# One exponential for three late score tiles of a pair, and the first heads' loads spread over the projections, in a four-layer graph network

## The chip, the cores and the metric

The kernel runs on one core of a Trainium2 chip. The metric is the device time of one execution in microseconds; the time before is 11191.26 us, the median of three runs (11190.45 to 11191.84).

## The reference

`x` is [3327, 128] and `adj` a 0/1 matrix [3327, 3327]. Four layers follow each other, each as `x = x + layer(relu(layernorm(x)), adj)`. Layer 1, a graph attention with 128 heads of 8 features, takes most of the time:

```python
q = (x @ Wq.T).reshape(d, n, h)      # d = 128 heads, n = 3327, h = 8
k = (x @ Wk.T).reshape(d, n, h)
v = (x @ Wv.T).reshape(d, n, h)
a = jnp.einsum('dnh,dmh->dnm', q, k) * scale
a = a + spatial_encoding + edge_encoding      # both are adj
a = jax.nn.softmax(a, axis=2)
out = jnp.einsum('dnm,dmh->dnh', a, v)
out = out.reshape(n, h * d)
return out @ Wo.T
```

So each head has a 3327 x 3327 matrix of scores, to which twice `adj` is added before the exponential. The other layers are products with `adj`, a GRU cell and a nearest-neighbour step.

## The kernel before, in words

**Projections (lines 421 to 510).** For each of 26 row blocks of 128 nodes TensorE multiplies by Wq, Wk and Wv (L464, L471), ScalarE copies each result into a staging tile (`qk_st` L466, `v_st` L474), and SP's queue stores it to memory (`store`, L440). The heads are taken in 32 groups of four. For the first groups `Parting` (L359 on) reads q and k back, splits each value into a rounded high part and a rest on GpSimd, and stores both parts (`kt`, `qt`), so that a score can be a product of 32 contraction rows: high and low parts of eight features. A list `early` holds such steps; after each row block from the third on one step is taken from it. Among them stand, as one step each, the loads of the first group (`load_heads(0, 0)`: eight times `k_in` and `q4`, then four times `v4`), and all 13 exponentials of `adj` (`exp_of`, L347), and then the steps that rearrange keys (`key_pair`, L419). Each `v_st` gets its column of ones by a GpSimd memset (L473). In this part a scheduler places the instructions; the program's order is not kept.

**Attention (lines 519 to 631).** The query nodes are cut in 7 chunks of 476 (the last 471). For each chunk and each group of four heads, 26 row tiles t of 128 keys are gone through; a `step` is one (chunk, group, t). The order here is written by hand (`manual_schedule`) and kept by every engine.

In `scores` each step makes four tiles [128 keys, up to 476 queries], one for each head, by matmuls on the four row groups of 32 rows of the array (L547). Twice `adj` comes in by one of three ways, a letter for each head:

```python
WAYS = ("DDDI", "DDIG")            # for even and odd t
PLACES = ((0, 1, 2, 5), (3, 4, 6, 7))
```

D: VectorE adds `a2` (twice adj) to the scores and writes to `p8` (L552); these scores are in tiles `early`, one PSUM bank each, four buffers. I: TensorE adds it in PSUM by a matmul with twice the identity (L550). G: GpSimd multiplies the exponential by the exponential of twice adj, `e_a` (L555). I and G scores are in a tile `late`, read by ScalarE's exponential (L553). An even step has one late score (tile `late1`, one bank), an odd step two (`late2`, two banks). After an odd step one wide exponential goes over the five D places of the pair (L557), in place. `p8` has eight places of 476 for a pair of steps and three buffers.

`weigh` (L564) multiplies each tile of `p8` by the values, on the four column groups, and adds up in one PSUM bank `acc` over t; each fp32 product is two matmul instructions, so a step has eight. It runs four steps behind the scores (`ahead = 4`). After the last t VectorE copies `acc` out (L573). PSUM is full: `acc` 1 bank, `late1` 1, `late2` 2, `early` 4.

On TensorE a step stands as: late scores, early scores, identity, the weighing of four steps ago. Beside it, in t 4 to 25, run the loads of the next group on SP's queue and its key rearrangement on GpSimd.

Of the kernel before, what the change touches and what calls it, by code (L numbers as in the profile page):

```python
# [8 lines left out]
F32 = mybir.dt.float32  # L9
# [18 lines left out]
E = 8  # L28
# [26 lines left out]
def kernel(  # L55
# [285 lines left out]
    def even(c):  # L341
        w = q_chunks[c][1]
        return w + w % 2

    def exp_of(a2, c):
        e = e_pool.tile([P, QW], F32, name="e")
        nc.scalar.activation(e[:, : even(c)], a2[:, : even(c)], AF.Exp)  # L347
        return e
# [40 lines left out]
                if t == 11:  # L389
                    self.store(side)  # L390

    def load_heads(c, g):
        q0, w = q_chunks[c]
        k_in = kq.tile([P, NP], F32, name="k_in", bufs=1)
        q4 = kq.tile([P, QW], F32R, name="q4")
        v4 = kq.tile([P, 4, T, EA], F32, name="v4")
        nc.gpsimd.memset(k_in[:, N:], 0.0)
        if w % 2:
            nc.gpsimd.memset(q4[:, w : w + 1].bitcast(F32), 0.0)
        for i in range(4):  # L400
# [5 lines left out]
        for i in range(4):  # L406
            n0 = (4 * g + i) * N
            nc.sync.dma_start(
                v4[:, i].rearrange("p t e -> p (t e)"),
                vd[n0 : n0 + NP, :].rearrange("(p t) e -> p (t e)", t=T),  # L410
            )
        return k_in, q4, v4, []

    def key_pair(heads):
# [7 lines left out]
    with tc.tile_pool(name="l1", bufs=1) as pool, tc.tile_pool(name="l1_ps", bufs=3, space=PSUM) as ps:  # L422
        w_st = pool.tile([D, 3, NH * E], F32, name="w_st")
        for i, w in enumerate((wq, wk, wv)):
            nc.gpsimd.dma_start(w_st[:, i, :], w)
        zero = pool.tile([HL, NH], F32, name="zero")
        nc.vector.memset(zero, 0.0)
        nc.gpsimd.dma_start(vd[N * NH : N * NH + 1, :], zero[:1, :EA])
        for end in (qf, kf):
            nc.gpsimd.dma_start(end[:E, N * NH :], zero[:E])  # L430

        with tc.tile_pool(name="l1_ln", bufs=1) as ln, tc.tile_pool(name="l1_tp", bufs=2, space=PSUM) as tps:
            h, done = layernorm_relu(ln)
            done(T)
            hT = transposed(pool, tps, h, "hT")
        st = ctx_st.enter_context(tc.tile_pool(name="l1_st", bufs=4))

        def store(dst, src, r, kp):
            for p0, p1 in ((0, kp),) if kp == P else ((0, 112), (112, kp)):
                nc.sync.dma_start(dst[r * P + p0 : r * P + p1], src[p0:p1])  # L440


        assert 7 * N + NP <= 2 * P * NH
        early = []
        for g in range(2):
            part = Parting(g)
            for side in range(2):
                early.append(lambda part=part: (part.load(0), part.load(1)) if part.lo[0] is None else None)
                early.append(lambda part=part, side=side: [part.part(side, i) for i in range(4)] and part.store(side))
        first, e_first = [], []  # L450
        early.append(lambda: first.extend(load_heads(0, 0)))
        ahead_part = Parting(2)
        early.append(lambda: (ahead_part.load(0), ahead_part.load(1)))
        early.append(lambda: e_first.extend(exp_of(a, 0) for a in a_first[1::2]))
        early += [lambda: (key_pair(first), key_pair(first))] * (T // 4)
        if T // 2 % 2:
            early.append(lambda: key_pair(first))
        for r in range(T):
            kp = rows_of(r)
            lhs = hT[:, r * P : r * P + kp]  # L460
            for i, (dst, mx) in enumerate(((qf, q_max), (kf, k_max))):
                pp = ps.tile([P, 2, 512], F32, name="pp", bufs=2)
                for c in range(2):
                    nc.tensor.matmul(pp[:kp, c, :], lhs, w_st[:, i, c * 512 : c * 512 + 512], start=True, stop=True)  # L464
                s = st.tile([P, E * NH], F32, name="qk_st")
                nc.scalar.activation(s[:kp], pp[:kp].rearrange("p a b -> p (a b)"), AF.Copy, scale=D**-0.5 if i == 0 else 1.0)  # L466
                nc.vector.tensor_reduce(mx[:kp, r : r + 1], s[:kp], AX.X, ALU.max, apply_absolute_value=True)
                store(dst[:E].rearrange("e (r c) -> r e c", c=NH), s.rearrange("p (e c) -> p e c", c=NH), r, kp)
            pp = ps.tile([P, 2, 512], F32, name="pp", bufs=2)
            for c in range(2):  # L470
                nc.tensor.matmul(pp[:kp, c, :], lhs, w_st[:, 2, c * 512 : c * 512 + 512], start=True, stop=True)  # L471
            s = st.tile([P, NH, EA], F32, name="v_st")
            nc.gpsimd.memset(s[:, :, E : E + 1], 1.0)  # L473
            nc.scalar.copy(s[:kp, :, :E], pp[:kp].rearrange("p a (c e) -> p (a c) e", e=E))  # L474
# [44 lines left out]
    with tc.tile_pool(name="at_in", bufs=1) as a_pool, tc.tile_pool(name="at_p", bufs=3) as p_pool, tc.tile_pool(  # L519
# [13 lines left out]
            q0, w = q_chunks[c]  # L533
            nc.sync.dma_start(adj16[t][:, q0 : q0 + w], a2[:, :w])

        def scores(step, heads, a2, e_a, p8):
            c, _, t = step
            we = even(c)
            _, q4, _, pairs = heads
            ways, places = WAYS[t % 2], PLACES[t % 2]  # L540
            n_d = ways.count("D")
            late = ps.tile([P, 4 - n_d, 512], F32, name=f"late{4 - n_d}")
            early = [ps.tile([P, 512], F32, name="early", bufs=4) for _ in range(n_d)]
            for i in (*range(n_d, 4), *range(n_d)):
                r = slice(32 * i, 32 * i + 32)
                sp = early[i] if i < n_d else late[:, i - n_d]
                nc.tensor.matmul(sp[:, :we], pairs[t // 2][r, t % 2, :], q4[r, :we], start=True, stop=ways[i] != "I")  # L547
            for i in range(4):
                if ways[i] == "I":
                    nc.tensor.matmul(late[:, i - n_d, :we], two_i, a2[:, :we], start=False, stop=True)  # L550
            for i in range(n_d):
                nc.vector.tensor_tensor(p8[:, places[i], :we], early[i][:, :we], a2[:, :we], op=ALU.add)  # L552
            nc.scalar.activation(p8[:, places[n_d] : places[3] + 1, :we], late[:, :, :we], AF.Exp)  # L553
            if ways[3] == "G":
                nc.gpsimd.tensor_tensor(p8[:, places[3], :we], p8[:, places[3], :we], e_a[:, :we], op=ALU.mult)  # L555
            if t % 2:
                nc.scalar.activation(p8[:, :5, :we], p8[:, :5, :we], AF.Exp)  # L557

        def weigh(step, v4, p8):
            c, g, t = step  # L560
# [17 lines left out]
        with tc.manual_schedule(engines=engines):  # L578
# [7 lines left out]
            for j, step in enumerate(steps):  # L586
# [6 lines left out]
                        a_t, a_next = a_next, []  # L593
                        e_t, e_next = e_next, []
                if t % 2 == 0:
                    p8 = p_pool.tile([P, 8, QW], F32, name="p8")
                scores(step, heads, a_t[t], e_t[t // 2], p8)
                begun[j] = (step, heads[2], p8)
                if j >= ahead:
                    weigh(*begun.pop(j - ahead))  # L600
                if t == min(4, T // 2) and more:
                    coming = load_heads(*groups[n])
                if c == 0 and g + 2 < n_groups:
# [506 lines left out]
```

## Time and profile before

| | |
|---|---|
| median of the runs | 11191.26 us |
| the profiled execution | 11195.14 us |
| its span, first to last instruction | 11193.4 us |
| granted TensorE clock, mean | 0.989 |
| busy: TensorE / ScalarE / VectorE / GpSimd | 97% / 91% / 83% / 54% |
| VectorE's adds (L552) | 14560, 646 ns each |
| ScalarE's wide exponentials (L557) | 2912, 2599 ns each |
| ScalarE's late exponentials (L553) | 5824, 1378 ns of 952 elements, 971 ns of 476 |
| TensorE's weighing (L564) | 46592 instructions, 564 ns each |

Times come from one profiled execution. PE is TensorE, PEld its weight loads, DVE VectorE, ACT ScalarE, POOL GpSimd and SP the queue that issues transfers. A line gives the source line, the engine, the operation, output<-input with partitions x elements, how often it ran, and then the busy time in us and the mean of one in ns, and the idle time before it with what ended that. In the timeline the first column is the start, the second how long the merged instructions took. Instructions of one engine overlap in these records: the next starts before the last has ended, so the pace of an engine is read from start to start.

### The profile page before, as it was taken

The page shows a single profiled execution, that of the slowest core. Times are in us where ns is not written, and L with a number is a line of the kernel's source. Part 1 is how long each engine was busy: PE and PEld are TensorE (multiplying, and loading weights), DVE is VectorE, ACT ScalarE, POOL GpSimd, SP SyncE. Part 2 cuts the span into 40 slices and gives each one's busy share as a digit, 9 for nine tenths or more (in the row PEclk, how much of TensorE's full clock was granted, in tenths as well). Part 3 has the DMA queues.
Part 4 walks back from the last instruction along what each step waited for, and adds up shares of the span by engine and source line. Part 5 has one row for each costly group of instructions (what it writes and reads, how often), then busy time and mean ns, then how long its engine had stood idle before and what let it go on. Part 6 is the DMA issues. An engine that isn't in the chain of part 4 may idle for free. (4 is left out here: it accounts for less than half of the span.)

```text
span 11193.4 us, 209350 instructions
## 1 busy us (share of the span) xinstructions
PE 10850.5 (97%) x79530; PEld 3005.9 (27%) x79530; DVE 9343.1 (83%) x15429; ACT 10199.3 (91%) x9152; POOL 6016.3 (54%) x6964
## 2 busy tenths in 40 slices
PE   9899999999999999999999999999999999999996
PEld 4322222222222222222222222222222222222453
DVE  8588888888888888888888888888888888888656
ACT  0399999999999999999999999999999999999522
POOL 0277777555555555555555555555555555555203
PEclk9899999999999999999999999999999999999998
DMA  7755554333333333333333333333333332333432
GB/s 264 238 129 120 123 127 109 65 64 64 68 64 62 67 66 63 68 65 61 68 66 63 66 66 61 67 66 61 66 66 61 66 63 55 61 58 58 135 113 97
DMA packets 417541, 942.25 MB, mean 84 GB/s; under 512 B 67936, under 2 KB 345937, under 8 KB 380940
## 3 DMA queue, kind: packets, MB, share of 16 engines
q1 hardware_dynamic: 412762, 918.98, 37.4%
q8 instruction: 627, 10.27, 0.4%
q0 software_dynamic: 3760, 9.78, 0.3%
q14 instruction: 392, 3.21, 0.1%
HBM read 788.78 MB, written 139.71 MB: 83 GB/s over the span
## 5 line engine op out<-in xcount | busy, mean ns | idle before, releaser
L552 DVE TENSOR_TENSOR p<-early,a 128x476 f32<-128x476 f32 (+1 forms) x14560 | 8426.4, 646 | 1369.4 <-PE early L547 1297.5
L557 ACT ACTIVATE p<-p 128x2380 f32<-128x2380 f32 (+1 forms) x2912 | 7568.4, 2599 | 0.4
L564 PE MATMUL acc<-p,v 128*9 128x476 f32 (+1 forms) x46592 | 5748.5, 564 | 15.3 <-ACT p L557 1.4
L553 ACT ACTIVATE p<-late 128x476 f32<-128x476 f32 (+1 forms) x5824 | 5315.4, 1175 | 13.8 <-DMA q<-qt 10.2
L555 POOL TENSOR_TENSOR p<-p,e 128x476 f32<-128x476 f32 (+1 forms) x2912 | 3528.1, 1212 | 3204.3 <-ACT p L553 2998.6
L547 PE MATMUL late<-q,k 32*128 32x476 f32 (+1 forms) x8736 | 2798.2, 478 | 99.5 <-ACT p L553 39.7
L547 PE MATMUL early<-q,k 32*128 32x476 f32 (+1 forms) x14560 | 2843.6, 478 | 9.4 <-DVE p L552 9.4
L419 POOL CAST k<-k_in 128x256 fp32r<-128x256 f32 x2912 | 1936.5, 697 | 886.4 <-DMA k_in<-kt 339.4
L547 PEld LDWEIGHTS late<-q,k 32*128 32x128 f32 x8736 | 1065.4, 181 | 4890.4 <-ACT p L553 4186.2
L550 PE MATMUL late<-a,two_i 128*128 128x476 bf16 (+1 forms) x5824 | 2180.8, 374 | 0.0
L547 PEld LDWEIGHTS early<-q,k 32*128 32x128 f32 x14560 | 1113.0, 181 | 9.9 <-DVE p L552 9.9
L564 PEld LDWEIGHTS acc<-p,v 128*9 128x9 f32 x46592 | 695.2, 88 | 1272.6 <-issue 1185.8
L550 PEld LDWEIGHTS <-two_i 128*128 128x128 bf16 x5824 | 556.2, 96 | 1329.0 <-issue 1329.0
L189 ACT COPY agg<-agg_ps 128x512 f32<-128x512 f32 x15 | 8.2, 591 | 485.5 <-PE agg_ps L204 290.6
L230 PE MATMUL agg_ps<-a,part 128*128 128x512 bf16 (+1 forms) x1092 | 227.0, 369 | 4.3 <-ACT agg L928 3.2
L272 POOL TENSOR_SCALAR a<-a_in 128x476 bf16<-128x476 f32 (+2 forms) x156 | 221.1, 1417 | 0.5
L272 POOL TENSOR_SCALAR a<-a 128x476 bf16<-128x476 f32 (+1 forms) x26 | 36.4, 1400 | 288.1 <-DMA a<-in_adjT_dram 288.1
L923 PE MATMUL sp<-yT,hT 128*128 128x512 f32 (+1 forms) x364 | 170.7, 610 | 12.3 <-ACT agg L928 6.4
L204 PE MATMUL agg_ps<-a,h 128*128 128x512 f32 (+2 forms) x364 | 148.2, 570 | 26.2 <-DVE h L164 26.2
L573 DVE COPY o<-acc 105x476 f32<-105x476 f32 (+1 forms) x224 | 144.5, 645 | 4.6 <-PE acc L564 4.6
L204 PE MATMUL agg_ps<-a,x 128*128 128x512 f32 (+2 forms) x364 | 145.3, 562 | 0.6 <-ACT x L318 0.6
L230 PEld LDWEIGHTS <-part 128*128 128x128 f16 x1092 | 108.6, 99 | 117.7 <-issue 10.3
(236 smaller groups left out, 2592.0 us busy)
## 6 DMA issues: line engine op xcount, KB each, us to landing
k_in<-kt SPq DMA_DIRECT2D x1792, 207.9 KB
v<-vd SPq DMA_DIRECT2D x896, 117.0 KB
a<-in_adjT_dram SPq DMA_DIRECT2D x50, 1663.5 KB
a<-adj SPq DMA_DIRECT2D x78, 831.8 KB
q<-qt SPq DMA_DIRECT2D x1536, 29.8 KB
a_in<-in_adjT_dram SPq DMA_DIRECT2D x125, 238.0 KB
adj<-a SPq DMA_DIRECT2D x156, 119.0 KB
vd<-v_st SPq DMA_DIRECT2D x25, 576.0 KB
```

Source lines behind the costliest of these rows:

```text
L204: nc.tensor.matmul(acc[c][:, :w], lhs[:kp, t, :], a[:kp, c0 : c0 + w], start=(t == 0), stop=(t == T - 1))
L230: nc.tensor.matmul(acc[c][:, :w], part[:, t, :], a[:, c0 : c0 + w], start=(t == 0 and i == 0), stop=(t == T - 1 and i == len(parts) - 1),)
L272: nc.gpsimd.tensor_scalar(a2[:kp, :w], a, 2.0, None, op0=ALU.mult)
L419: nc.gpsimd.tensor_copy(k, slots(k_in)[:, t : t + 2, :])
L547: nc.tensor.matmul(sp[:, :we], pairs[t // 2][r, t % 2, :], q4[r, :we], start=True, stop=ways[i] != "I")
L550: nc.tensor.matmul(late[:, i - n_d, :we], two_i, a2[:, :we], start=False, stop=True)
L552: nc.vector.tensor_tensor(p8[:, places[i], :we], early[i][:, :we], a2[:, :we], op=ALU.add)
L553: nc.scalar.activation(p8[:, places[n_d] : places[3] + 1, :we], late[:, :, :we], AF.Exp)
L555: nc.gpsimd.tensor_tensor(p8[:, places[3], :we], p8[:, places[3], :we], e_a[:, :we], op=ALU.mult)
L557: nc.scalar.activation(p8[:, :5, :we], p8[:, :5, :we], AF.Exp)
L564: nc.tensor.matmul(acc[32 * i : 32 * i + EA, :w], v4[:kp, i, t, :], p8[:kp, PLACES[t % 2][i], :w], start=(t == 0), stop=(t == T - 1),)
L923: nc.tensor.matmul(sp[:, c0 : c0 + w], slots(zT)[:, t, :], z2T[:, cols], start=True, stop=False)
```

## The change

Scores are made for a pair of steps at once. The three late scores of a pair go to one PSUM tile `late` of three banks (one buffer), and one exponential of 3 x 476 elements reads it, in place of one of 476 and one of 952. On TensorE a pair now stands as: the even step's three early scores, the three late scores, two identities, the odd step's two early scores, then the weighing of two steps (eight matmuls each). GpSimd's multiplication is a function of its own, `times_e`, called at the odd step.

In the projections the loads of the first group are given as eight pieces: four that load a head's `k_in` and `q4` parts, one for each row block, and four that load a head's `v4`, each with a step of two `key_pair` calls and two exponentials of adj. An empty step of the list is dropped. Four `v_st` tiles with names of their own get their ones once, ahead of the loop.

```diff
-    def load_heads(c, g):
+    def load_heads(c, g, pieces=None):
...
+        for f in (scored, weighted):
+            for i in range(4):
+                if pieces is None:
+                    f(i)
+                else:
+                    pieces.append(lambda f=f, i=i: f(i))
         return k_in, q4, v4, []
...
-        first, e_first = [], []
-        early.append(lambda: first.extend(load_heads(0, 0)))
         ahead_part = Parting(2)
         early.append(lambda: (ahead_part.load(0), ahead_part.load(1)))
-        early.append(lambda: e_first.extend(exp_of(a, 0) for a in a_first[1::2]))
-        early += [lambda: (key_pair(first), key_pair(first))] * (T // 4)
-        if T // 2 % 2:
-            early.append(lambda: key_pair(first))
+        pieces, e_first = [], []
+        first = load_heads(0, 0, pieces)
+        early += pieces[:4]
+        key_steps = -(-(T // 2) // 2)
+        for i in range(key_steps):
+            def step(i=i):
+                for f in pieces[4 + i : 5 + i if i < key_steps - 1 else None]:
+                    f()
+                for n in (2 * i, 2 * i + 1):
+                    if n < T // 2:
+                        key_pair(first)
+                        e_first.append(exp_of(a_first[2 * n + 1], 0))
+            early.append(step)
+        v_sts = [st.tile([P, NH, EA], F32, name=f"v_st{i}", bufs=1) for i in range(4)]
+        for s in v_sts:
+            nc.gpsimd.memset(s[:, :, E : E + 1], 1.0)
...
-            s = st.tile([P, NH, EA], F32, name="v_st")
-            nc.gpsimd.memset(s[:, :, E : E + 1], 1.0)
+            s = v_sts[r % 4]
...
-        def scores(step, heads, a2, e_a, p8):
+        def scores(step, heads, a2s):
...
-            late = ps.tile([P, 4 - n_d, 512], F32, name=f"late{4 - n_d}")
-            early = [ps.tile([P, 512], F32, name="early", bufs=4) for _ in range(n_d)]
...
-            nc.scalar.activation(p8[:, places[n_d] : places[3] + 1, :we], late[:, :, :we], AF.Exp)
-            if ways[3] == "G":
-                nc.gpsimd.tensor_tensor(p8[:, places[3], :we], p8[:, places[3], :we], e_a[:, :we], op=ALU.mult)
-            if t % 2:
-                nc.scalar.activation(p8[:, :5, :we], p8[:, :5, :we], AF.Exp)
+            p8 = p_pool.tile([P, 8, QW], F32, name="p8")
+            late = ps.tile([P, 3, 512], F32, name="late")
+            def score(odd, i, sp):
+                r = slice(32 * i, 32 * i + 32)
+                nc.tensor.matmul(sp[:, :we], pairs[t // 2][r, odd, :], q4[r, :we], start=True, stop=WAYS[odd][i] != "I")
+            def early(odd):
+                for i in range(WAYS[odd].count("D")):
+                    sp = ps.tile([P, 512], F32, name="early", bufs=4)
+                    score(odd, i, sp)
+                    nc.vector.tensor_tensor(p8[:, PLACES[odd][i], :we], sp[:, :we], a2s[odd][:, :we], op=ALU.add)
+            early(0)
+            lates = [(odd, i) for odd in range(2) for i in range(4) if WAYS[odd][i] != "D"]
+            for n, (odd, i) in enumerate(lates):
+                score(odd, i, late[:, n])
+            for n, (odd, i) in enumerate(lates):
+                if WAYS[odd][i] == "I":
+                    nc.tensor.matmul(late[:, n, :we], two_i, a2s[odd][:, :we], start=False, stop=True)
+            early(1)
+            nc.scalar.activation(p8[:, 5:, :we], late[:, :, :we], AF.Exp)
+            nc.scalar.activation(p8[:, :5, :we], p8[:, :5, :we], AF.Exp)
+            return p8
...
-                scores(step, heads, a_t[t], e_t[t // 2], p8)
+                    p8 = scores(step, heads, a_t[t : t + 2])
+                else:
+                    times_e(step, p8, e_t[t // 2])
                 begun[j] = (step, heads[2], p8)
-                if j >= ahead:
-                    weigh(*begun.pop(j - ahead))
+                if t % 2:
+                    for i in (j - 1 - ahead, j - ahead):
+                        if i >= 0:
+                            weigh(*begun.pop(i))
```

More of the change, by code (lines that the diff above doesn't have):

```diff
@@ L399, in load_heads, with scored @@
             nc.gpsimd.memset(q4[:, w : w + 1].bitcast(F32), 0.0)
-        for i in range(4):
+        def scored(i):
             n0 = (4 * g + i) * N
@@ L405, in load_heads, with weighted @@
                 nc.sync.dma_start(q4[r : r + HL, :w].bitcast(F32), dram(qt, E * j * GP + n0 + q0, [[0, 2], [GP, E], [1, w]]))
-        for i in range(4):
+        def weighted(i):
             n0 = (4 * g + i) * N
@@ L447 @@
             for side in range(2):
-                early.append(lambda part=part: (part.load(0), part.load(1)) if part.lo[0] is None else None)
+                if side == 0:
+                    early.append(lambda part=part: (part.load(0), part.load(1)))
                 early.append(lambda part=part, side=side: [part.part(side, i) for i in range(4)] and part.store(side))
-        first, e_first = [], []
-        early.append(lambda: first.extend(load_heads(0, 0)))
         ahead_part = Parting(2)
         early.append(lambda: (ahead_part.load(0), ahead_part.load(1)))
-        early.append(lambda: e_first.extend(exp_of(a, 0) for a in a_first[1::2]))
-        early += [lambda: (key_pair(first), key_pair(first))] * (T // 4)
-        if T // 2 % 2:
-            early.append(lambda: key_pair(first))
+        pieces, e_first = [], []
[14 more added lines that the diff above has]
+            nc.gpsimd.memset(s[:, :, E : E + 1], 1.0)
         for r in range(T):
@@ L539, in scores @@
             _, q4, _, pairs = heads
-            ways, places = WAYS[t % 2], PLACES[t % 2]
-            n_d = ways.count("D")
-            late = ps.tile([P, 4 - n_d, 512], F32, name=f"late{4 - n_d}")
-            early = [ps.tile([P, 512], F32, name="early", bufs=4) for _ in range(n_d)]
-            for i in (*range(n_d, 4), *range(n_d)):
-                r = slice(32 * i, 32 * i + 32)
-                sp = early[i] if i < n_d else late[:, i - n_d]
-                nc.tensor.matmul(sp[:, :we], pairs[t // 2][r, t % 2, :], q4[r, :we], start=True, stop=ways[i] != "I")
@@ L548, in scores @@
[L548 to L553, printed above, removed]
-            if ways[3] == "G":
-                nc.gpsimd.tensor_tensor(p8[:, places[3], :we], p8[:, places[3], :we], e_a[:, :we], op=ALU.mult)
@@ new lines, in scores @@
+            early(0)
+            lates = [(odd, i) for odd in range(2) for i in range(4) if WAYS[odd][i] != "D"]
+            for n, (odd, i) in enumerate(lates):
+                assert PLACES[odd][i] == 5 + n
+                score(odd, i, late[:, n])
[4 more added lines that the diff above has]
+            nc.scalar.activation(p8[:, 5:, :we], late[:, :, :we], AF.Exp)
@@ L559, in weigh, with times_e @@
+            nc.scalar.activation(p8[:, :5, :we], p8[:, :5, :we], AF.Exp)
+            return p8
+        def times_e(step, p8, e_a):
+            we = even(step[0])
+            assert WAYS[1][3] == "G"
+            nc.gpsimd.tensor_tensor(p8[:, PLACES[1][3], :we], p8[:, PLACES[1][3], :we], e_a[:, :we], op=ALU.mult)
         def weigh(step, v4, p8):
@@ L595 @@
                 if t % 2 == 0:
-                    p8 = p_pool.tile([P, 8, QW], F32, name="p8")
-                scores(step, heads, a_t[t], e_t[t // 2], p8)
+                    p8 = scores(step, heads, a_t[t : t + 2])
+                else:
+                    times_e(step, p8, e_t[t // 2])
                 begun[j] = (step, heads[2], p8)
-                if j >= ahead:
-                    weigh(*begun.pop(j - ahead))
+                if t % 2:
+                    for i in (j - 1 - ahead, j - ahead):
+                        if i >= 0:
+                            weigh(*begun.pop(i))
                 if t == min(4, T // 2) and more:
```

## The prediction

> **What bounds the kernel now.** I read the page's busy shares first, then busy time by stretch, the groups by form, and the timeline of two pairs of steps in the middle. A pair is two row tiles t, t+1; there are 7 chunks x 32 groups x 13 = 2912 of them.
>
> ```profile
> core 0: us, PE busy (x) PEld busy (x) DVE busy (x) ACT busy (x) POOL busy (x), PEclk, DMA share, GB/s
> 382.00:566.00 184.00, 150.15 (x312) 63.60 (x310) 63.80 (x54) 79.59 (x78) 32.70 (x68) 0.88 0.88 264
> 576.00:10476.00 9900.00, 9784.58 (x75704) 2407.52 (x75704) 8533.98 (x14784) 9893.06 (x8814) 5812.77 (x6734) 1.00 0.36 71
> ```
>
> The stretch 576 to 10476 is the attention: 9900 us, 3.40 a pair. ScalarE is busy 9893 of it. TensorE looks as busy (9785), but its ends are modelled, so the share does not say which of the two is the limit. The groups by form do:
>
> ```profile
> L557 ACT ACTIVATE p<-p 128x2380 f32<-128x2380 f32 x2496 | 6491.5, 2601 | 0.4
> L553 ACT ACTIVATE p<-late 128x952 f32<-128x952 f32 x2496 | 3439.5, 1378 | 3.6 <-PE late L550 3.5
> L553 ACT ACTIVATE p<-late 128x476 f32<-128x476 f32 x2496 | 2424.5, 971 | 10.2 <-DMA q<-qt 10.2
> L547 PE MATMUL late<-q,k 32*128 32x476 f32 x7488 | 2399.8, 478 | 90.9 <-ACT p L553 38.9 <-ACT v_st L474 1.1
> ```
>
> The exponentials have practically no idle time before them (0.4, 3.6, 10.2 us in all), while TensorE's late scores wait on ScalarE. ScalarE is the limit, and TensorE is just behind it:
>
> ```profile
> 5000.93 0.47 PE L547 MATMUL late<-q,k 32*128 32x476 f32 x1
> 5001.03 0.57 PE L547 MATMUL early<-q,k 32*128 32x476 f32 x3
> 5001.26 2.55 ACT L557 ACTIVATE p<-p 128x2380 f32<-128x2380 f32 x1
> 5001.62 2.91 DVE L552 TENSOR_TENSOR p<-early,a 128x476 f32<-128x476 f32 x5 [0.53 <-PE early L547]
> 5003.34 1.79 ACT L553 ACTIVATE p<-late 128x476 f32<-128x476 f32 x2
> 5003.48 0.99 PE L564 MATMUL acc<-p,v 128*9 128x476 f32 x8
> 5004.40 0.48 PE L547 MATMUL late<-q,k 32*128 32x476 f32 x1
> 5004.63 2.57 ACT L557 ACTIVATE p<-p 128x2380 f32<-128x2380 f32 x1
> 5004.81 0.37 PE L550 MATMUL late<-a,two_i 128*128 128x476 bf16 x1
> 5005.12 0.99 PE L564 MATMUL acc<-p,v 128*9 128x476 f32 x8
> ```
>
> Start to start, ScalarE's pair is 2.08 (wide exponential, 5001.26 to 5003.34) + 1.29 (the two late ones) = 3.37. TensorE's step is 0.92 (weighing, 5003.48 to 5004.40) + 0.41 (scores) + 0.31 (identity) = 1.64, so 3.28 a pair if nothing held it. VectorE does its five adds in 2.91 and then idles 0.5.
>
> **Saved on ScalarE.** 952 and 476 elements cost 1378 and 971 ns, so 476 cost 407. The two late ones take 1.29 together; three times 0.407 would be 1.22, and three times the 0.40 by which their starts differ 1.19. So one exponential of 1428 elements takes about 1.25, and the removed instruction is worth 0.04 to 0.06 a pair: ScalarE's floor falls from 3.37 to 3.32, at best 2912 x 0.05 = 146 us. The Trainium skill (ScalarE: Activation LUTs, "What ACT_TABLE_LOAD costs") gives 186 ns fixed per ACTIVATE with some 93 overlapped; by that estimate it would be 93 ns a pair, 271 us. The trace's starts decide.
>
> **Added on TensorE.** Before, each step has one round of four scores side by side (row groups 0 to 3), one identity, one weighing. After, a pair is: three early and one late score; then the two odd late ones, whose row groups 2 and 3 are taken, so a second round; two identities; then the odd step's two early scores, a third round; then 16 weighing matmuls. Three rounds instead of two, but four changes of shape instead of six. These rows price it:
>
> ```profile
> 566.66 0.37 PE L550 MATMUL late<-a,two_i 128*128 128x476 bf16 x1
> 566.97 0.48 PE L547 MATMUL late<-q,k 32*128 32x476 f32 x2
> 579.77 0.77 PE L547 MATMUL early<-q,k 32*128 32x476 f32 x2
> 580.47 0.58 PE L550 MATMUL late<-a,two_i 128*128 128x476 bf16 x1
> 589.66 0.48 PE L547 MATMUL late<-q,k 32*128 32x476 f32 x2
> 590.08 0.38 PE L550 MATMUL late<-a,two_i 128*128 128x476 bf16 x1
> 591.59 2.19 ACT L557 ACTIVATE p<-p 128x2380 f32<-128x2380 f32 x1
> ```
>
> Scores to identity is 0.70 at half clock (579.77) and 0.42 at full clock (589.66): 0.28 scales with the clock, about 0.14 is the change of shape. Likewise identity to next is 0.31, of which about 0.20 is streaming (its 375 ns fall by 2 for 4 columns fewer). The pair after, term by term:
> - first to second score round: no row. Between 0.20 (streaming alone) and 0.42 (as dear as a change of shape); I take the 0.28 that scales with the clock.
> - second round to identity 0.42; identity to identity 0.20 to 0.31, I take 0.21 (same shape); identity to scores 0.31 (566.66 to 566.97).
> - two scores to weighing: no row; 0.28 if this change were free, 0.53 if as dear as weighing to scores (0.92 less two rounds of 0.40, so 0.11 more); I take 0.42, the row for leaving scores.
> - two weighings in a row: 0.80 + 0.92 = 1.72, at most 1.84.
>
> Sum 0.28 + 0.42 + 0.21 + 0.31 + 0.42 + 1.72 = 3.36, against 3.28; ends 3.13 and 3.83.
>
> The trace shows no second matmul on a row group whose predecessor is still streaming with other late weights; the nearest is the second half of the weighing, 0.40 after the first with 0.40 of streaming, so no load is exposed. The Trainium skill (TensorE: Matmul & The Clock Gate, "Part 3: Packing small matmuls") says that a weight load overlaps matmuls in flight only where the row group differs; with the 181 ns load exposed the second round would be 0.38, 0.10 more than my term, and the loop below 0.03 longer.
>
> **Added: a longer loop.** Before, late scores had two tiles (one and two banks), so one could be filled while the other was read, and the odd early scores followed freely. Now one tile of three banks serves the pair, with one buffer. Behind its wait stand, on TensorE's in-order queue, the identities, the odd early scores and the weighing; VectorE's last two adds, and with them the wide exponential, wait for those. The loop:
> - late tile free to the late scores: 0.05, the gap in the trace from a late exponential's end to scores that waited for it.
> - late scores to the next pair's first scores, TensorE: 3.36.
> - those to the wide exponential: 0.55 to the first add (median over the stretch; 0.59 in the rows above, 5001.03 to 5001.62), 2.91 for five adds, 0.03 to the release of ScalarE: 3.49.
> - the wide exponential from a standing start 2.19 (591.59), then the late one 1.25, which frees the tile two pairs further: 3.44.
>
> Sum 0.05 + 3.36 + 3.49 + 3.44 = 10.34 over three pairs: 3.45 a pair. That is above ScalarE's floor of 3.32 and TensorE's own 3.36, so the freed time on ScalarE becomes waiting, chiefly before the wide exponential. Against 3.40: 0.05 x 2912 = 146 us more. Pool's multiplication (1.2 us) is one pair off its user, and weighing lags two pairs as before: nothing. VectorE's copy of acc (0.64, once in 13 pairs) falls in its idle time.
>
> **The projections.** The part 382 to 566 has two stops that the first heads' loads make, when 16 of them, then four of v, stand ahead of the stores on SP's queue:
>
> ```profile
> 473.22 3.78 PE L471 MATMUL pp<-w_st,hT 128*128 128x512 f32 x4 [5.62 <-ACT qk_st L466]
> 497.25 3.78 PE L471 MATMUL pp<-w_st,hT 128*128 128x512 f32 x4 [15.66 <-ACT qk_st L466]
> ```
>
> Spread over eight row blocks they are at best absorbed (21 us), at worst each block stops a few us for its four loads, since SP's three stores (1.2 + 1.5 + 2.2 us on its queue) nearly fill a block of 5.15. DMA is 88% busy there, so I take -10 (range -21 to +15). The 13 exponentials of adj keep their places in ScalarE's queue in the built program, so that part does nothing; 22 memsets fewer on an idle Pool are nothing too.
>
> **Sum.** The profiled execution took 11195.1 us (span 11193.4); + 146 - 10 gives 11331. The median of the runs, 11191.3, is 4 less: 11327.
>
> **Rivals.**
> 1. *Faster: the saving is kept.* The loop without TensorE's part is 6.98, so with TensorE's sum under 3 x 3.40 - 6.98 = 3.22 it is under 3.40 and the sign turns. All low ends (3.13) give 10.11 / 3 = 3.37, -87; if the loop does not close at all, ScalarE's 3.32 plus what lies between 3.37 and 3.40 today, 3.35, gives -146. With -10: 11035 to 11095. For it: ScalarE has been the limit, and changes of shape fall from six to four. Against: 0.5 of idle on VectorE is all the slack there is. 0.22.
> 2. *TensorE becomes the bound.* From a sum of 3.49 (half of 6.98) its own cycle passes the loop. At 3.55 a pair: 0.15 x 2912 - 10 = +427, 11618; the high end, 3.83, would be 12430. For it: three of six terms have no row, and all err upwards. 0.18.
> 3. *Nothing to see:* loop within 0.01 of 3.40, 11180 to 11210. 0.06.
>
> My forecast (3.41 to 3.53, 11210 to 11560) has 0.54. The range 11080 to 11630 leaves out most of rival 1's far end and rival 2 above 3.55. About 0.2% (22 us) is what a measurement can tell from no change. Faster 0.22, same 0.07, slower 0.71.
>
> **What would show it.** Right: starts of wide exponentials about 3.45 apart, not evenly but in a rhythm of three, idle before them put down to VectorE's adds, ScalarE's busy time in the attention well below 99%. Wrong: late exponential plus wide one back to back at 3.32 to 3.35 (rival 1); TensorE's blocks without a gap at 3.5 or more (rival 2); or a second round at 0.4.

## The result, and the profile after

The changed kernel takes 11379.59 us (median of 4 runs, 11376.42 to 11381.49), the kernel before, run beside it, 11191.55 (11190.45 to 11194.51): 1.0167 times as long, 95% interval 1.015 to 1.0185. The profiled execution has a span of 11379.8 us, at a mean clock of 0.99. The forecast was 11327, 136 more than before: the sign and the range held, and 52 of the 188 us were missing.

Busy time by stretch, after (the attention ran from 576 to 10476 before):

```profile
core 0: us, PE busy (x) PEld busy (x) DVE busy (x) ACT busy (x) POOL busy (x), PEclk, DMA share, GB/s
382.00:559.00 177.00, 151.41 (x316) 63.42 (x318) 63.79 (x54) 80.09 (x79) 26.52 (x49) 0.92 0.91 275
570.00:10664.00 10094.00, 10085.59 (x75703) 3286.43 (x75703) 8542.85 (x14784) 10026.95 (x5902) 5815.27 (x6734) 1.00 0.35 70
```

ScalarE runs 2912 instructions fewer (5902 against 8814) and the stretch is about 190 us longer all the same. Its busy time is no guide to what binds: it is 10027 of 10094, though ScalarE now waits. In shift_four (below), where nothing holds it, the wide exponential starts 1.24 us after the late one, whose record still runs; here it starts 1.35 after it (medians), and the late one's record of 1.34 fills that time. Between starts of wide exponentials the mean is 3.465 us a pair, before 3.398; 0.067 x 2912 = 195. The attention begins 7 us earlier, so 188 remain. The typical pair (median) went from 3.371 to 3.446.

Groups by form, after, and the queue of waits between 600 and 10600 us (us in total, times, longest):

```profile
L587 ACT ACTIVATE p<-p 128x2380 f32<-128x2380 f32 x2496 | 5468.4, 2191 | 53.8 <-DVE p L575 11.9
L586 ACT ACTIVATE p<-late 128x1428 f32<-128x1428 f32 x2496 | 3354.8, 1344 | 12.3 <-DMA vd<-v_st 11.2 <-POOL lo_q L376 1.1
```

```profile
PEld early L569 <- DVE p L575: 3130.8, 5010, 0.8
```

One late exponential of 1428 elements stands where two stood. The wait that the forecast looked for, idle ScalarE ahead of the wide exponential put down to VectorE, is 11.9 us in all. The wait itself is there: in 97% of the pairs the wide exponential starts 0.03 after the end of the pair's fifth add. It shows as the 0.11 more from start to start, not as idle time. What is put down to VectorE as idle time now is TensorE's early scores, 5010 times: they wait for an add to have read an early bank. Before, this was 9.9 us in all (groups by form, before):

```profile
L547 PEld LDWEIGHTS early<-q,k 32*128 32x128 f32 x14560 | 1113.0, 181 | 9.9 <-DVE p L552 9.9
```

Most of the 3131 us is no stop: the weight loads of a pair's first scores come up to 0.8 us after the loads before them anyhow, while the matmuls of the weighing still run. The timeline of two pairs shows the part that is one:

```profile
5003.35 1.34 ACT L586 ACTIVATE p<-late 128x1428 f32<-128x1428 f32 x1
5004.61 0.48 PE L569 MATMUL early<-q,k 32*128 32x476 f32 x3
5004.71 2.19 ACT L587 ACTIVATE p<-p 128x2380 f32<-128x2380 f32 x1
5004.75 0.69 PE L569 MATMUL late<-q,k 32*128 32x476 f32 x3
5005.23 2.89 DVE L575 TENSOR_TENSOR p<-early,a 128x476 f32<-128x476 f32 x5 [0.56 <-PE early L569]
5005.37 0.57 PE L584 MATMUL late<-a,two_i 128*128 128x476 bf16 x2
5005.88 0.54 PE L569 MATMUL early<-q,k 32*128 32x476 f32 x2
5006.34 1.78 PE L600 MATMUL acc<-p,v 128*9 128x476 f32 x16
5006.80 1.34 ACT L586 ACTIVATE p<-late 128x1428 f32<-128x1428 f32 x1
5008.06 0.49 PE L569 MATMUL early<-q,k 32*128 32x476 f32 x3
5008.15 2.19 ACT L587 ACTIVATE p<-p 128x2380 f32<-128x2380 f32 x1
```

A pair makes five early scores on four banks, so the odd step's second early score needs the bank of the pair's own first one. Follow it: first early score 5004.61; its add begins at 5005.23 (0.62 later) and takes 0.65; the bank is free 0.06 after that, at 5005.94. There the second of the two odd early scores starts (one score takes 0.48, the pair of them 0.54, so it starts 0.06 after 5005.88). The weighing follows 0.40 later and takes 1.72, to the next pair's first score at 5008.06. 0.62 + 0.65 + 0.06 + 0.40 + 1.72 = 3.45: a loop within a single pair, over VectorE's first add and TensorE's order. It holds in the whole trace: the second odd score starts 0.054 to 0.055 after the end of the pair's first add (5th to 95th percentile of 2769 pairs).

### The profile page after: what moved, and what is told of

Read it like the earlier page. It is cut to its first block, busy times and chain, and to the rows that moved or that the text cites. A ratio compares the mean times of both kernels' runs of the same rounds, so it can differ in the third digit from the quotient of the medians.

```text
span 11379.8 us, 206391 instructions
## 1 busy us (share of the span) xinstructions
PE 11169.0 (98%) x79530; PEld 3882.7 (34%) x79530; DVE 9351.8 (82%) x15429; ACT 10333.7 (91%) x6240; POOL 6011.4 (53%) x6942
## 4 chain that ended last, share of the span: by engine, by line
PE 90%; ACT 4%; issue 3%; DVE 1%; DMA 1%; POOL 1%; SPq 0%; DVEq 0%; ACTq 0%; POOLq 0%
PE acc L600 42%; PE early L569 22%; PE late L584 12%; PE late L569 8%; PE agg_ps L204 2%; ACT p L586 1%; ACT p L587 1%; PE agg_ps L230 1%; PE pp L488 1%; POOL rows L993 0%; DMA qf<-qk_st 0%; PE yp L777 0%; ACT e L347 0%; PE pp L495 0%; PE mp L315 0%
## 5 line engine op out<-in xcount | busy, mean ns | idle before, releaser
L587 ACT ACTIVATE p<-p 128x2380 f32<-128x2380 f32 (+1 forms) x2912 | 6372.6, 2188 | 63.0 <-DVE p L575 13.3
L600 PE MATMUL acc<-p,v 128*9 128x476 f32 (+1 forms) x46592 | 5191.8, 563 | 0.7 <-ACT p L587 0.7
L586 ACT ACTIVATE p<-late 128x1428 f32<-128x1428 f32 (+1 forms) x2912 | 3909.5, 1343 | 12.3 <-DMA vd<-v_st 11.2
L569 PE MATMUL early<-q,k 32*128 32x476 f32 (+1 forms) x14560 | 3018.3, 479 | 11.4 <-DVE p L575 10.2
L569 PEld LDWEIGHTS early<-q,k 32*128 32x128 f32 x14560 | 1276.4, 181 | 3484.5 <-DVE p L575 3167.6
L569 PE MATMUL late<-q,k 32*128 32x476 f32 (+1 forms) x8736 | 2022.0, 409 | 5.9 <-ACT p L586 0.3
L600 PEld LDWEIGHTS acc<-p,v 128*9 128x9 f32 x46592 | 994.3, 90 | 2338.6 <-issue 2333.8
L584 PE MATMUL late<-a,two_i 128*128 128x476 bf16 (+1 forms) x5824 | 1674.5, 369 | 0.0
L569 PEld LDWEIGHTS late<-q,k 32*128 32x128 f32 x8736 | 852.4, 183 | 29.4 <-ACT p L586 29.4
L584 PEld LDWEIGHTS <-two_i 128*128 128x128 bf16 x5824 | 330.5, 97 | 965.5 <-issue 965.5
```

The costliest lines, as they stand in the source:

```text
L569: nc.tensor.matmul(sp[:, :we], pairs[t // 2][r, odd, :], q4[r, :we], start=True, stop=WAYS[odd][i] != "I")
L584: nc.tensor.matmul(late[:, n, :we], two_i, a2s[odd][:, :we], start=False, stop=True)
L586: nc.scalar.activation(p8[:, 5:, :we], late[:, :, :we], AF.Exp)
L600: nc.tensor.matmul(acc[32 * i : 32 * i + EA, :w], v4[:kp, i, t, :], p8[:kp, PLACES[t % 2][i], :w], start=(t == 0), stop=(t == T - 1),)
```

## The experiments

Theory A was the forecast's: the late tile's single buffer closes a loop over three pairs. Theory B is the one just read: the early banks close a loop over one pair. Times are medians of device time, each ratio is to the kernel before on the same chip, with its 95% interval.

**Which half of the change.** The kernel before with only the projections of the change (loads_only), and with only its attention (pairs_only):

```diff
 # loads_only, against before
-        early.append(lambda: first.extend(load_heads(0, 0)))
...
+        first = load_heads(0, 0, pieces)
+        early += pieces[:4]
...
+            s = v_sts[r % 4]
 # pairs_only, against before
-        def scores(step, heads, a2, e_a, p8):
+        def scores(step, heads, a2s):
...
+            nc.scalar.activation(p8[:, 5:, :we], late[:, :, :we], AF.Exp)
+            nc.scalar.activation(p8[:, :5, :we], p8[:, :5, :we], AF.Exp)
```

> Only the change in the projections: the first heads' loads in eight pieces, the four v_st tiles; the attention as before. In the changed kernel's trace the first wide exponential starts at 572.5 us instead of 579.1. Theory (the attention makes the whole loss, the projections a small gain): 7 us faster than before, 11185. Rival (the pieces cost as much as they save once the attention is as before): within 3 us of before.

> Only the change in the attention, the projections as before. Theory: 2912 x (3.465 - 3.398) = 195 us slower than before, 11386, and wide exponentials 3.446 us apart in the middle. Rival (the projections' new order delays the attention, for instance by where buffers come to lie): clearly less than 195.

Measured: loads_only 11191.04 against 11197.09, ratio 0.9995 (0.9986 to 1.0004): not told apart from nothing, though its trace has the first wide exponential at 570.79 us, before 579.10. pairs_only 11390.22, 1.0173 (1.0157 to 1.0188), 3.446 a pair as in after. The whole loss is in the attention.

**Merged exponential or TensorE's order.** order_only keeps after's order on TensorE, but gives the late scores two tiles again and two exponentials:

```diff
-            late = ps.tile([P, 3, 512], F32, name="late")
+            late1 = ps.tile([P, 1, 512], F32, name="late1")
+            late2 = ps.tile([P, 2, 512], F32, name="late2")
+            late = [late1[:, 0], late2[:, 0], late2[:, 1]]
...
-            nc.scalar.activation(p8[:, 5:, :we], late[:, :, :we], AF.Exp)
+            nc.scalar.activation(p8[:, 5:6, :we], late1[:, :, :we], AF.Exp)
+            nc.scalar.activation(p8[:, 6:, :we], late2[:, :, :we], AF.Exp)
```

> The changed kernel with two late tiles (one and two banks) and two late exponentials as before, but TensorE's new order by pairs kept. Theory (a loop over three pairs: late tile, TensorE, five adds, wide and late exponential): the second score round need not wait for the first to be let go, the loop falls by some 0.24 / 3 to 3.37, and the next limit shows: the odd step's second early score, which waits for the first add's bank (1.29 after the pair's first scores, then 0.41 + 1.72), 3.42 a pair, or ScalarE's 3.385. So 3.42: about 11290, 90 less than the changed kernel, though it has 2912 exponentials more. Rival (one exponential for three tiles is what costs, by its wait for all three): back to before, 11185. Rival (TensorE's own sequence without any wait is the bound): as the changed kernel, 11380.

Measured: 11385.79, 1.0169 (1.0153 to 1.0184). The expectation failed: the pace is 3.446 to 3.448, as in after. Timeline of order_only, TensorE and ScalarE:

```profile
5003.25 0.49 PE L571 MATMUL early<-q,k 32*128 32x476 f32 x3
5003.26 0.69 PE L571 MATMUL late<-q,k 32*128 32x476 f32 x3
5003.89 0.57 PE L586 MATMUL late<-a,two_i 128*128 128x476 bf16 x2
5004.39 0.66 PE L571 MATMUL early<-q,k 32*128 32x476 f32 x2
5004.98 1.78 PE L603 MATMUL acc<-p,v 128*9 128x476 f32 x16
5006.69 0.48 PE L571 MATMUL early<-q,k 32*128 32x476 f32 x3
```

```profile
5003.35 2.19 ACT L590 ACTIVATE p<-p 128x2380 f32<-128x2380 f32 x1
5006.79 2.19 ACT L590 ACTIVATE p<-p 128x2380 f32<-128x2380 f32 x1
```

Late scores start 0.01 after the early ones (0.14 in after), so they no longer wait for ScalarE, and nothing is gained. The two odd early scores take 0.66 instead of 0.48: the second waits 0.18, and again starts 0.055 after the end of the first add (5th to 95th percentile 0.055 to 0.056), as theory B has it. The pace of after is set by this order alone; merging the exponentials neither costs nor gains anything in it.

**ScalarE's order.** act_shift puts the wide exponential of a pair behind the late one of the next pair, so that the late tile comes free without waiting for VectorE's adds. That opens theory A's loop:

```diff
             nc.scalar.activation(p8[:, 5:, :we], late[:, :, :we], AF.Exp)
-            nc.scalar.activation(p8[:, :5, :we], p8[:, :5, :we], AF.Exp)
+            wide()
+            to_widen.append((p8, we))
             return p8
...
+        def wide():
+            for q8, w in to_widen:
+                nc.scalar.activation(q8[:, :5, :w], q8[:, :5, :w], AF.Exp)
+            to_widen.clear()
...
+            wide()
```

> The changed kernel, but on ScalarE the wide exponential of a pair stands behind the late exponential of the next pair. So the late tile comes free without waiting for five adds, and the loop over three pairs is open. Theory: the pace falls from 3.446 to the next limit, the early banks' 3.42, and the copies of acc no longer show: 11280, 100 less than the changed kernel, still slower than before. Rival (nothing but that loop holds it, TensorE's sequence without waits is 3.29): ScalarE's 3.33, 11040, faster than before. Rival (TensorE's sequence is the bound at 3.446 whatever ScalarE does): 11380.

Measured: 11377.36, 1.0161 (1.0145 to 1.0176); again missed, again 3.445 a pair. Two ways of opening theory A's loop leave the time where it was. Theory A is not what binds after. Both times the number of the rival came, 11380 for a TensorE sequence that is the bound by itself. Against that rival stands that the second odd score follows the first add's end by 0.055 here too, however early the first odd score starts; the next two runs decide it.

**Opening theory B's loop, with and without theory A's.** shift_four is act_shift, four_only is after, each without the odd step's second early score (the add of that head reads the first head's tile), so that a pair needs four banks for four scores:

```diff
                 for i in range(WAYS[odd].count("D")):
-                    sp = ps.tile([P, 512], F32, name="early", bufs=4)
-                    score(odd, i, sp)
+                    if not (odd and i):
+                        sp = ps.tile([P, 512], F32, name="early", bufs=4)
+                        score(odd, i, sp)
                     nc.vector.tensor_tensor(p8[:, PLACES[odd][i], :we], sp[:, :we], a2s[odd][:, :we], op=ALU.add)
```

> The shifted exponential, and the odd step's second early score is not made: the add of that head reads the first head's tile, so this head's sums are wrong in odd tiles; all other instructions stay. Four early tiles a pair in four banks, so no score waits for an add of its own pair. Theory (after the three-pair loop the early banks are the limit): the pace falls from 3.42 to ScalarE's 3.33 to 3.35, 11040 to 11100, faster than before. Rival (TensorE's sequence is the bound in itself): as with the shift alone, since two scores or one make the same round.

> The changed kernel with ScalarE's order as it is, but the odd step's second early score not made (its add reads the first head's tile, so this head's sums are wrong in odd tiles): four early tiles a pair in four banks. Theory (two loops of nearly one length: the early banks' of one pair, 3.446, binds, and the one over three pairs stands just under it): the bank loop opens and the other shows, 0.05 + 3.25 + 3.55 + 3.43 = 10.28 over three, 3.43 a pair: 11330. Rival (only the bank loop exists): ScalarE's 3.33, as with the shifted exponential, 11030.

Measured: shift_four 11031.13, 0.9857 (0.9841 to 0.9874); four_only 11322.0, 1.0118 (1.0102 to 1.0133). Both came as expected. Timeline of shift_four, TensorE and then ScalarE's wide exponentials:

```profile
5000.03 0.48 PE L569 MATMUL early<-q,k 32*128 32x476 f32 x3
5000.04 0.69 PE L569 MATMUL late<-q,k 32*128 32x476 f32 x3
5000.67 0.58 PE L585 MATMUL late<-a,two_i 128*128 128x476 bf16 x2
5001.17 0.48 PE L569 MATMUL early<-q,k 32*128 32x476 f32 x1
5001.58 1.78 PE L609 MATMUL acc<-p,v 128*9 128x476 f32 x16
5003.30 0.48 PE L569 MATMUL early<-q,k 32*128 32x476 f32 x3
```

```profile
5002.62 2.18 ACT L596 ACTIVATE p<-p 128x2380 f32<-128x2380 f32 x1
5005.94 2.19 ACT L596 ACTIVATE p<-p 128x2380 f32<-128x2380 f32 x1
5009.26 2.20 ACT L596 ACTIVATE p<-p 128x2380 f32<-128x2380 f32 x1
```

With both loops open TensorE's pair is 3.27 in these lines (0.64 + 0.50 + 0.41 + 1.72), and ScalarE's 3.32 is the limit: the removed instruction is worth 0.05 a pair where nothing takes it back. ScalarE's timeline in four_only, where only theory B's loop is open:

```profile
5028.72 2.19 ACT L588 ACTIVATE p<-p 128x2380 f32<-128x2380 f32 x1 [0.20 <-DVE p L576]
5032.06 2.18 ACT L588 ACTIVATE p<-p 128x2380 f32<-128x2380 f32 x1
5035.38 2.18 ACT L588 ACTIVATE p<-p 128x2380 f32<-128x2380 f32 x1
5039.02 2.19 ACT L588 ACTIVATE p<-p 128x2380 f32<-128x2380 f32 x1 [0.21 <-DVE p L576]
```

Here is the rhythm of three that the forecast described, every third wide exponential waiting for VectorE: the steps are 3.34, 3.32 and 3.64, 10.30 over three pairs. Elsewhere in the trace the wait is spread over more steps and leaves little idle time (over 0.1 us before 301 of the 2912), but three pairs take as long, 10.29 at the median, 3.43 a pair. Theory A's loop exists. It stands just under theory B's 3.446, which hides it in after.

**Lengthening VectorE's part.** A spare add of 238 columns is put between the even and the odd step's adds of a pair: in after (extra_dve), in act_shift (shift_extra), in before (before_extra, where it adds the even step's piece of adj to itself).

```diff
+        spare = a_pool.tile([P, XW], F32, name="spare")
...
+            nc.vector.tensor_tensor(spare[:, :XW], a2s[0][:, :XW], a2s[1][:, :XW], op=ALU.add)
```

> The changed kernel with one more VectorE instruction a pair (a sum of two pieces of adj, 238 columns, into a spare tile) between the even step's three adds and the odd step's two. It should take some 0.28 us. Theory (loop over three pairs, VectorE passed once): the pace grows by a third of it, 0.09, some 270 us: 11650. Rival (TensorE's sequence is the bound; VectorE idles 0.55 a pair): no change, 11380. Rival (VectorE's adds are passed once in every pair): the whole 0.28, 815 us: 12195.

> The same extra VectorE instruction, with the wide exponential behind the next pair's late exponential. Theory (the loop over three pairs is open, VectorE's 3.1 a pair is under the pace): within 50 us of the kernel with the shifted exponential alone. Rival (the shift does not open the loop): 270 us more than that kernel.

> The kernel before with the same extra VectorE instruction, once a pair behind the even step's adds. Theory (ScalarE is the bound, VectorE idles 0.5 a pair): within 30 us of before, 11191. Rival (VectorE's adds are on the path already): up to 270 us more.

Measured: extra_dve 11851.47, 1.0593 (1.0575 to 1.0611); shift_extra 11567.28, 1.0332 (1.0315 to 1.035); before_extra 11434.15, 1.0219 (1.0202 to 1.0236). All three are dearer than expected, so the totals decide nothing. The size of the probe was off: the spare add takes 0.40 us where GpSimd is idle, and more where GpSimd is at work. Timeline of before_extra, VectorE's spare adds and GpSimd:

```profile
5017.00 1.02 DVE L557 TENSOR_TENSOR spare<-a 128x238 f32<-128x238 bf16 x1
5031.07 0.40 DVE L557 TENSOR_TENSOR spare<-a 128x238 f32<-128x238 bf16 x1
```

```profile
5016.55 1.21 POOL L560 TENSOR_TENSOR p<-p,e 128x476 f32<-128x476 f32 x1
5029.53 1.21 POOL L560 TENSOR_TENSOR p<-p,e 128x476 f32<-128x476 f32 x1 [1.55 <-ACT p L558]
```

The first spare add starts inside a multiplication of GpSimd, which ends at 5017.76, and ends 0.26 after it. The second starts with GpSimd idle. In the whole trace, 1635 spare adds start with GpSimd idle and take 0.40 (5th to 95th percentile alike); 1277 start inside an operation of GpSimd, with a median of 0.61 and 95th percentile of 1.24, and end 0.27 after that operation (median). With GpSimd idle the next add starts 0.31 after the spare one, since the records overlap: that is the probe's plain price. The steps that begin at the third to seventh pair of a group show it: extra_dve runs there in a rhythm of three, 3.445, 3.478, 3.688, together 10.61, which is theory A's 10.29 and 0.32 more; shift_extra keeps act_shift's 3.44 and before_extra before's 3.37. There all three do what theory A's loop asks of them; in those of the ninth and tenth pairs they do not (3.60 and 3.76 in before_extra). So these runs agree with that loop, but only for a part of each group.

**Versions that might keep the saving.** half_weigh is act_shift with one step's weighing between the identities and the odd early scores, so that the banks have time:

```diff
                     nc.tensor.matmul(late[:, n, :we], two_i, a2s[odd][:, :we], start=False, stop=True)
+            between()
             early(1)
...
-                    for i in (j - 1 - ahead, j - ahead):
-                        if i >= 0:
-                            weigh(*begun.pop(i))
+                    if j >= ahead:
+                        weigh(*begun.pop(j - ahead))
```

> The shifted wide exponential, and one step's weighing moved between the identities and the odd early scores, so that the time until the bank is free is filled with work. Nothing is left out. Theory (the wait for the bank is 0.13 to 0.17 a pair, but the move adds a change of shape, 0.11): TensorE's sequence is 0.66 + 0.21 + 0.31 + 0.92 + 0.41 + 0.92 = 3.41, 100 less than the changed kernel, 11280. Rival (a change of shape costs nothing once the weights are loaded in time): 3.32, ScalarE's pace, 11030.

Measured: 11601.31, 1.0367 (1.0351 to 1.0383), far off. Its waits name the cause:

```profile
PEld acc L609 <- ACT p L596: 1548.3, 2824, 1.0
```

The weighing, now half a pair earlier, waits in nearly every pair for the wide exponential that act_shift had put a pair later: it starts 0.05 after that one's end (5th to 95th percentile alike). Each edit moved one end of the same product towards the other.

four_one leaves the exponentials in after's order, deals out the ways anew and weighs between two blocks of scores: four early scores at once, a weighing, then three late ones and the fifth early one.

```diff
-    WAYS = ("DDDI", "DDIG")
-    PLACES = ((0, 1, 2, 5), (3, 4, 6, 7))
+    WAYS = ("DDDI", "DIGD")
+    PLACES = ((0, 1, 2, 5), (4, 6, 7, 3))
...
-            early(0)
+            early((0, 0), (0, 1), (0, 2), (1, 3))
+            between()
+            late = ps.tile([P, 3, 512], F32, name="late")
...
+            early((1, 0))
```

> One late exponential for three tiles, but other heads in VectorE's share: four early scores at the even step (even heads 0 to 2, odd head 3), at the odd step the three late ones and one early on four different row groups. So two rounds of four as before, TensorE's sequence without waits 0.42 + 0.92 + 0.42 + 0.21 + 0.31 + 0.92 = 3.18. Nothing is left out. Theory (early banks): the fourth score of a pair waits for the fifth add of the pair before, 0.62 + 4 x 0.56 + 0.65 + 0.07 = 3.58 after that pair's first scores; with 3.18 this gives (3.58 + 3.18) / 2 = 3.38 a pair and some 0.015 for the copies of acc: 11180, within 40 of before. Rival (ScalarE's saving is kept): 3.33, 11030. Rival (the three-tile exponential's wait binds here as well): 3.43 or more, 11330.

Measured: 11193.15 over 11 runs, 1.0003 (0.9994 to 1.0012): 186 us of the loss are back, and the kernel before is just met. Timeline of four_one:

```profile
5004.77 0.49 PE L568 MATMUL early<-q,k 32*128 32x476 f32 x4
5005.19 0.99 PE L601 MATMUL acc<-p,v 128*9 128x476 f32 x8
5006.11 0.49 PE L568 MATMUL late<-q,k 32*128 32x476 f32 x3
5007.04 0.99 PE L601 MATMUL acc<-p,v 128*9 128x476 f32 x8
5007.95 0.86 PE L568 MATMUL early<-q,k 32*128 32x476 f32 x4
```

Pairs alternate between 3.317, ScalarE's floor, and about 3.415. In one pair the four early scores start together (0.49); in the next they are spread (0.86) and wait for banks. Each group also has one pair of 3.653, at the copy of `acc`. The mean is 3.400, against before's 3.398.

four_one_copy moves that copy to ScalarE, between the late and the wide exponential:

```diff
-                nc.vector.tensor_copy(o4[: 96 + EA, :w], acc[: 96 + EA, :w])
+                nc.scalar.copy(o4[: 96 + EA, :w], acc[: 96 + EA, :w])
```

> The kernel with four and one early scores, and the copy of acc at the end of a group is made by ScalarE, between the late and the wide exponential, instead of VectorE. Nothing is left out. In the trace of the four-and-one kernel the pair of that copy takes 3.65 instead of 3.37, 224 times. Theory (VectorE's adds and the early banks set the pace, ScalarE has 0.04 a pair to spare): that pair's 0.28 goes, ScalarE's copy of some 0.45 takes up 13 x 0.04 of slack: about 60 us less, 11130, faster than before. Rival (ScalarE cannot take 0.45 more a group): 11190, no change. Rival (the first weighing of the next group waits longer for acc): up to 224 x 0.3 us more, 11250.

Measured: 11251.14, 1.0057 (1.0043 to 1.007), the case that the expectation priced at 11250. Groups by line:

```profile
L604 PE MATMUL acc<-p,v 128*9 128x476 f32 (+1 forms) x46592 | 5754.8, 564 | 140.5 <-ACT o L613 138.0 <-POOL p L597 1.4 <-ACT p L592 1.1
```

TensorE's first weighing of the next group waits for the copy, queued on ScalarE behind an exponential (138 us). The step of the copy itself falls from 3.65 to 3.46, as expected, but the step before it rises from 3.41 to 3.84. No version with five early scores is measurably faster than the kernel before.

## Why the prediction was right, and where not

**ScalarE's saving: right.** 0.05 a pair was forecast, with a floor of 3.32; before's quiet pairs run at 3.369 and shift_four at 3.32. The estimate from the Trainium skill (ScalarE: Activation LUTs, "What ACT_TABLE_LOAD costs"), 93 ns, is nearly twice the 49 ns that these two paces give. Right too is where the freed time goes, into ScalarE's wait for VectorE's adds ahead of the wide exponential (0.11 a pair).

**TensorE's sequence: too long by 0.09.** shift_four has it without a wait, in the lines above: first scores to identities 0.64 (forecast 0.28 + 0.42), identities to odd early scores 0.50 (0.21 + 0.31), to the weighing 0.41 (0.42), weighing 1.72: 3.27 against 3.36. Most of the difference is in the two rounds of scores: the second starts 0.32 after the first (0.28), but the identity only 0.31 after that (0.42). The rule of the Trainium skill (TensorE: Matmul & The Clock Gate, "Part 3: Packing small matmuls"), by which a weight load overlaps matmuls in flight only where the row group differs, would make it 0.38 + 0.42 = 0.80 to the identities; the 0.64 does not show it, and the second round's loads begin 0.10 after the last score of the first round, whose record takes 0.48.

**The loop: one of two, and not the one that binds.** This is the step that failed. The forecast took TensorE's pair as running through once the late tile was free, and asked of the odd early scores only what stood ahead of them in the queue. Their banks were never counted: "the odd early scores followed freely" was said of before, and nothing of after. In the loop that it did name, a second term was off: the first add does not start 0.55 after the first early score, a median that before's trace does not give (0.59 in the rows shown, 0.65 at the median), but 0.62 after it, in four_only and in after. With 3.27, and 0.62 + 2.89 + 0.03 = 3.54, the named loop is 0.05 + 3.27 + 3.54 + 3.44 = 10.30, 3.43 a pair, and four_only shows 10.29. That loop alone gives 11322, in a kernel that makes one score less. The early banks make it 3.446, and 11380. That 3.446 and the forecast's 3.45 agree is chance: the forecast's loop came to it by one term 0.09 too long and one 0.07 too short, the kernel by 3.27 and 0.18 of waits on TensorE (in after 0.13 ahead of the late scores, 0.05 ahead of the second odd score).

**The comparison: 49 us.** The forecast set the bare pace of a loop, 3.45, against before's mean of 3.40, and so priced 146 us. A mean holds also the pairs that are longer than the rest: after has 26 us in the pairs behind a copy of `acc` (3.557 against 3.446, 218 times) and 28 us in the 78 pairs with an exponential of adj for the next chunk. Median against median it is 3.446 - 3.371 = 0.075, mean against mean 0.067: 195 us. The copy of `acc` that was to fall "in its idle time" is thus part of the same slip.

**The projections: right in size, not resolved.** -10 was forecast; the attention begins 7 us earlier in after, and loads_only cannot be told from before.

**The rivals.** The saving kept (1) is what both loops open would give, and shift_four reached it, at 11031. TensorE as the bound (2) did not come: its sequence is under ScalarE's floor. The signs to look for were half useful: wide exponentials 3.45 apart was right, the rhythm of three is absent from after, and the wait for VectorE's adds left no idle time, so that ScalarE's busy share stayed at 99%.

## What to carry to other kernels

When instructions of an in-order engine are moved closer together, count for each tile that it writes how many come between two releases and how many buffers there are: five scores on four banks were free while a weighing lay between them, and set the pace once they stood in one block. List every loop of the new order with its length, and open them one at a time on the chip: with lengths of 3.446 and 3.43, opening either one alone shows little or nothing. Where records overlap, read a wait from start to start: a busy share of 99% hid one of 0.11 in every pair. Compare a pace with a pace and a mean with a mean.

## What the runs showed of the hardware

A VectorE add with both inputs in SBUF takes 0.40 us for 238 columns of bf16 with GpSimd idle at its start, and 0.61 at the median (1.24 at the 95th percentile) inside an operation of GpSimd, whose end it then outlasts by 0.27. The Trainium skill (SBUF — State Buffer, "SBUF: two separate sides") describes such a lock between the two engines, for VectorE operations with two SBUF inputs against GpSimd operations that read SBUF; it fits the numbers, and was overlooked when the probe was sized. The kernel's own adds, which read one input from PSUM, keep 645 ns in after.
